# A selective scan on one core: order of the Softplus pair, place of the projections and of C

## The chip, the cores and the metric

The kernel runs on one core of a Trainium2 chip. A core has a TensorE for matrix products (PE in the profile; PEld is its weight load), a VectorE (DVE), a ScalarE (ACT), a GpSimd (POOL) and a SyncE (SP), which here only issues DMAs. Each engine works through its own list of instructions in order and waits at semaphores for the others. The metric is the time of the program on the device in microseconds (us).

## The reference

The input is `x` of shape (8, 384, 64, 64) in float32: 8 images of 384 channels. Two layers follow each other, both as `x = x + layer(group_norm(x))`.

- Layer 0 is a channel attention: three 1x1 convolutions and depthwise 3x3 convolutions for q, k and v, an attention between the channels of each of 8 heads, and an output projection.
- Layer 1 is a selective scan over the 4096 pixels in four directions (k = 0 to 3: by rows, by columns, and both reversed). The part that matters here, for each direction:

```python
x_dbl = jnp.einsum('bkdl,kcd->bkcl', xs, x_proj_weight)
dts, Bs, Cs = (x_dbl[:, :, :R], x_dbl[:, :, R:R + N], x_dbl[:, :, R + N:])   # R = 12, N = 16
dts = jnp.einsum('bkrl,kdr->bkdl', dts, dt_projs_weight)
dt = jax.nn.softplus(dts + dt_projs_bias[None, :, :, None])
# for each pixel, with 16 states for each of 384 channels:
dA = jnp.exp(dtt[..., None] * A)
h = h * dA + (dtt * ut)[..., None] * bt[:, :, None, :]
y = jnp.einsum('bkdn,bkn->bkd', h, ct)
```

The four directions are added, with a skip term `D * u`; a layer norm over the channels and a GELU end the layer.

## The kernel before

One image after the other, in three stages: `channel_attention`, `selective_scan`, `finish`. Only the scan is changed.

**Steps, pairs and periods.** A scan runs 32 steps for an image: 4 directions of 8 chunks of 512 pixels. In each step the 16 states are handled as 8 pairs (p = 0 to 7). The Python function `period(g)` writes the instructions of one pair; g counts pairs over all steps, so s = g // 8 is the step and p = g % 8 the pair. All instructions of the scan are pinned: on each engine they stand in the order in which the Python code writes them.

**What a period does.** Channels lie on the 128 partitions in three blocks (j = 0, 1, 2).

- ScalarE makes the decay `exp(dt * A)` for each of two states and three blocks: six `decay` instructions (line 449), each into one of two PSUM banks (`da`).
- GpSimd makes the input term `w * B`: two `drive` instructions (line 456), each for three blocks, one period ahead, from rows of B that `fetch` broadcast from DRAM three periods ahead.
- VectorE runs six `scan` instructions of 512 pixels (line 468). A decay bank comes free when the scan that read it has ended.
- TensorE turns the states of the pair before, so that pixels lie on partitions: eight `turn` groups of three 128x128 transposes (line 490), into the two banks of pool `ps_t`.
- Each turned block is multiplied by C and copied to SBUF by `apply_c` (lines 502 and 504). Most copies are on ScalarE; those in the set `on_dve` are on VectorE. A copy frees the bank that the transposes two further need.
- TensorE adds the copies up over pairs and states with `add_up`: three groups of four 384-column products (line 524), and a fourth group of twelve 128-column products (line 530), written one period later. In direction 0 the second pair adds the skip products as well (line 516).

**What a step needs besides.** `project(s, j)` makes dt, B and C for a chunk with three products of 512 columns into the one bank of pool `ps_m` (line 362); `lay_out` copies the result to SBUF (`xd`, line 370), writes B and C to DRAM and reads C back as rows (`cx`, eight DMAs on SP). `mingle_c` reorders `cx` on GpSimd, `turn_c` transposes it on TensorE into the bank of `ps_m` (`pct`, line 391), and `keep_c` copies it to SBUF on ScalarE (`ct`, line 399). The copies of the step's first pair read `ct`. In pair 1, called the burst, `step_matmuls` makes the inputs of Softplus for the next step: `pd` 0 into the bank of `ps_m`, `pd` 1 and 2 into the two banks of `ps_t` (line 416). `step_size` then runs three Softplus instructions on ScalarE (line 427), with a table load before and after them. `weigh` multiplies x by dt on GpSimd in pairs 2 to 4. In pair 1 VectorE also takes the finished sum of the step before (`take`), and SP stores it.

**Where these stand before.** The burst has copies 4, 5 and 6 on VectorE; pairs 4 and 7 have copy 3 there. Projections for step s + 2 stand in pairs 4, 5 and 6, between the second sum and transposes 6; `lay_out` of step s + 2 stands in pair 7. For step s + 1, `mingle_c` is in pair 2, `turn_c` in pair 3 and `keep_c` in pair 4.

[...]`ps_y` holds three (`py`), `ps_a` two (`da`), `ps_t` two, `ps_m` one.

Of the kernel before, what the change touches and what calls it, by code (L numbers as in the profile page):

```python
# [17 lines left out]
NJ = C // P  # L18
H = W = 64
L = H * W  # L20
CH = 512
# [8 lines left out]
XR = R + 2 * N  # L30
# [40 lines left out]
def tile_channel_attention_then_selective_scan(ctx: ExitStack, tc: tile.TileContext, a: dict):  # L71
# [224 lines left out]
    def selective_scan(b, x1, stats1):  # L296
# [10 lines left out]
        with ExitStack() as st:  # L307
# [8 lines left out]
            wx = wp.tile([P, NJ, K, XR], F32, name=f"wx{b}")  # L316
            nc.sync.dma_start(wx, a["x_proj"])

            with tc.tile_pool(name=f"sn{b}", bufs=1) as np_:
# [4 lines left out]
                for c in range(NCH):  # L324
                    for j in range(NJ):
                        s = x1[j][:, bass.ts(c, CH)]
# [11 lines left out]
            def view(t, k, c):  # L338

                if k % 2 == 0:  # L340
                    return t[:, bass.ts(c, CH)].rearrange("p (x y) -> p x y", y=W)
                return t.rearrange("p (h w) -> p w h", w=W)[:, bass.ts(c, CH // H), :]

            def split(t):
                return t.rearrange("p (x y) -> p x y", y=W)
# [5 lines left out]
            S = len(steps)  # L351
            wdts, pxs, xds, bc_ds, cts, dts, ws, bts = {}, {}, {}, {}, {}, {}, {}, {}

            def project(s, j):

                k, c = steps[s][:2]
                if j == 0:
                    if k not in wdts:
                        wdts[k] = work.tile([R, C], F32, tag="wdt", name=f"wdt{b}_{k}")
                        nc.sync.dma_start(wdts[k], a["dt_proj"][:, k, :])  # L360
                    pxs[s] = ps_m.tile([P, CH], F32, tag="m", name=f"px{b}_{s}")
                pin(nc.tensor.matmul(  # L362
                    split(pxs[s][:XR, :]), lhsT=wx[:, j, k, :], rhs=view(x1[j], k, c),
                    start=j == 0, stop=j == NJ - 1,
                ))

            def lay_out(s):

                xd = work.tile([XR, CH], F32, tag="xd", name=f"xd{b}_{s}")
                pin(nc.scalar.copy(xd, pxs.pop(s)[:XR, :]))  # L370
                bc_d = dram.tile([2 * N, CH], F32, tag="bcd", bufs=3, name=f"bcd{b}_{s}")
                nc.sync.dma_start(bc_d, xd[R:, :])

                cx = work.tile([NP * NQ, 2, HP], F32, tag="cx", name=f"cx{b}_{s}")
                for p in range(NP):
                    nc.sync.dma_start(
                        cx[p * NQ : (p + 1) * NQ],
                        bc_d[N + 2 * p : N + 2 * p + 2, :].rearrange("v (q l) -> q v l", l=HP),
                    )
                xds[s], bc_ds[s], cts[s] = xd, bc_d, cx  # L380
# [7 lines left out]
            def turn_c(s):  # L388

                pct = ps_m.tile([P, CH], F32, tag="m", name=f"pct{b}_{s}")  # L390
                pin(nc.tensor.transpose(
                    pct[:, : NP * NQ], cts[s].rearrange("r l v -> r (l v)"),
                    ident[: NP * NQ, : NP * NQ],
                ))
                cts[s] = pct

            def keep_c(s):
                ct = work.tile([P, NP * NQ], F32, tag="ct", name=f"ct{b}_{s}")
                pin(nc.scalar.copy(ct, cts[s][:, : NP * NQ]))
                cts[s] = ct  # L400
# [21 lines left out]
            def step_size(s, pds):  # L422
                k = steps[s][0]
                dts[s] = work.tile([P, NJ, CH], F32, tag="dt", name=f"dt{b}_{s}")
                ws[s] = work.tile([P, NJ, CH], F32, tag="w", name=f"w{b}_{s}")
                for j in range(NJ):
                    pin(nc.scalar.activation(  # L427
                        dts[s][:, j, :], pds[j], AF.Softplus, bias=small["dt_bias"][:, j, k : k + 1]
                    ))
# [147 lines left out]
                    move_y(s, t, True)  # L577

            for s in range(2):
                for j in range(NJ):  # L580
                    project(s, j)
                lay_out(s)
                if s == 0:
                    step_size(0, step_matmuls(0))
                    for j in range(NJ):
                        weigh(0, j)
                    for g in range(3):
                        fetch(g)
                    drive(0, 0)
                    drive(0, 1)  # L590
                    decay(0, 0, 0)
                    decay(0, 0, 1)
            mingle_c(0)
            turn_c(0)
            keep_c(0)

            def period(g):

                o, s, p = g - 1, g // NP, g % NP
                last = g == S * NP
                burst = p == 1 and s + 1 < S
                on_dve = {4, 5, 6} if burst else {3} if p in (4, 7) else set()
                taken = s - 1 if p == 1 and s > 0 else None

                def step(i):  # L610
                    if not last:
                        scan(g, *divmod(i, NJ))

                def next_decay(i):
                    if not last:
                        decay(g, *divmod(i + 2, NJ))

                def apply(q):
                    if o >= 0:
                        apply_c(o, q, nc.vector if q in on_dve else nc.scalar)  # L620

                def turned(q):
                    if o >= 0:
                        turn(o, q)

                def added(lb):
                    if o >= 0:
                        add_up(o, lb)

                def take_all():  # L630
                    if taken is not None:
                        for i in range(NJ):
                            take(taken, i)

                if not last:
                    h2s[g] = work.tile([P, NJ, CH, 2], F32, tag="h", bufs=3, name=f"h{b}_{g}")
                    if p == 2:
                        sum_of(s)
                if o >= 0:
                    keep_last(o)  # L640
                fetch(g + 3)
                drive(g + 1, 0)
                if p == 2 and s + 1 < S:
                    mingle_c(s + 1)
                if 2 <= p < 2 + NJ and s + 1 < S:
                    weigh(s + 1, p - 2)
                turned(0)
                turned(1)
                if o >= 1:
                    add_up(o - 1, NJ)  # L650
                apply(0)
                turned(2)
                step(0)
                next_decay(0)
                apply(1)
                turned(3)
                step(1)
                if not burst:
                    if p == 1:
                        take_all()  # L660
                    added(0)
                next_decay(1)
                apply(2)
                if burst:
                    pds = step_matmuls(s + 1)
                else:
                    turned(4)
                step(2)
                drive(g + 1, 1)
                next_decay(2)  # L670
                apply(3)
                if burst:
                    step_size(s + 1, pds)
                    step(3)
                    step(4)
                    take_all()
                    turned(4)
                    turned(5)
                    added(0)
                    apply(4)  # L680
                    turned(6)
                    apply(5)
                    turned(7)
                    added(1)
                    apply(6)
                    next_decay(3)
                    next_decay(4)
                    added(2)
                    step(5)
                    apply(7)  # L690
                    next_decay(5)
                    return
                turned(5)
                added(1)
                if 4 <= p < 4 + NJ and s + 2 < S:
                    project(s + 2, p - 4)
                if p == 7 and s + 2 < S:
                    lay_out(s + 2)
                if p == 3 and s + 1 < S:
                    turn_c(s + 1)  # L700
                if p == 4 and s + 1 < S:
                    keep_c(s + 1)
                apply(4)
                turned(6)
                step(3)
                next_decay(3)
                apply(5)
                turned(7)
                step(4)
                added(2)  # L710
                next_decay(4)
                apply(6)
                step(5)
                next_decay(5)
                apply(7)
# [51 lines left out]
    for b in range(B):  # L767
        x1, x1_d, stats1 = channel_attention(b)
# [51 lines left out]
```

## Time and profile before

| | before |
|---|---|
| time, median of 3 runs | 22354.12 us (22353.34 to 22354.86) |
| profiled execution, span | 22346.0 us |
| TensorE busy | 19355.1 us, 87% |
| VectorE busy | 19274.5 us, 86% |
| ScalarE busy | 17586.5 us, 79% |
| GpSimd busy | 15744.1 us, 70% |
| one scan instruction, VectorE (line 468, with a carry) | 1267 ns |
| one decay, ScalarE (line 449) | 700 ns |
| one copy, ScalarE (line 502) / VectorE (line 504) | 584 ns / 608 ns |
| one Softplus (line 427) / table load | 685 ns / 1283 ns |
| one projection product (line 362), two passes of 512 columns | 831 ns in the mean |

How to read it: the durations of following instructions on one engine overlap, so what an instruction costs its engine is the distance from start to start, which is shorter than its duration. Busy shares are over the whole span, which has three different stages for each image. In lists of groups and in the timeline, the bracket at the end is idle time of the engine just before the row, and what ended it. The stretch lists give, for each stretch, its length and the busy time (and count) of PE, PEld, DVE, ACT and POOL, then the granted TensorE clock, the DMA share and GB/s.

### The profile page before, as it was taken

To read this page: it belongs to the slowest core of one execution; us is meant where nothing else is said; L and a number is where in the kernel's file an instruction comes from. 1 tells how busy PE (TensorE), PEld (TensorE's weight loads), DVE (VectorE), ACT (ScalarE), POOL (GpSimd) and SP (SyncE) were. 2 spreads that over 40 slices of the span, in tenths; PEclk is the share of its full clock that TensorE was granted. 3 is DMA by queue.
4 is the path that set the end of the run, shared out by engine and by line. 5 is a ranking of instruction groups with operands and counts; after the bars stand their busy time and mean duration, and the time that the engine had idled before them with its cause. 6 is when DMAs were issued, how large, how long until landed. Compare 5 with 4: busy or idle time off the path is not lost.

```text
span 22346.0 us, 308970 instructions
## 1 busy us (share of the span) xinstructions
PE 19355.1 (87%) x113712; PEld 10323.1 (46%) x113712; DVE 19274.5 (86%) x16838; ACT 17586.5 (79%) x30794; POOL 15744.1 (70%) x7117
## 2 busy tenths in 40 slices
PE   7999879998799987999879998799987999879998
PEld 3544445444454444544445444454444544445444
DVE  7889878898789987889878998789987899878998
ACT  3999839998399983999839998399983999839998
POOL 0888718887188871888718887188871888718887
PEclk8999989999899998999989999899998999989999
DMA  1222312223122231222312223122231222312223
GB/s 51 77 86 86 109 46 77 86 87 109 46 78 85 87 113 43 77 86 86 113 43 77 86 87 113 42 78 85 87 114 42 77 85 87 114 41 77 86 86 103
DMA packets 872157, 1807.27 MB, mean 81 GB/s; under 512 B 123504, under 2 KB 513264, under 8 KB 861424
## 3 DMA queue, kind: packets, MB, share of 16 engines
q1 hardware_dynamic: 808464, 1658.85, 23.2%
q10 hardware_dynamic: 62176, 128.66, 1.7%
q8 instruction: 896, 14.68, 0.3%
q14 instruction: 621, 5.09, 0.1%
HBM read 1468.39 MB, written 318.77 MB: 80 GB/s over the span
## 4 chain that ended last, share of the span: by engine, by line
ACT 54%; PE 31%; DVE 10%; issue 3%; DMA 2%; POOL 1%; SPq 0%; ACTq 0%; POOLq 0%; DVEq 0%
ACT hc L502 27%; ACT da L449 23%; PE pt L490 10%; PE py L524 7%; PE px L362 4%; DVE v L196 4%; DVE ak L196 3%; PE pp L286 2%; ACT L427 1%; ACT dt L427 1%; DVE h L468 1%; PE py L530 1%; PE pa L245 1%; PE ptq L214 1%; PE py L516 1%
## 5 line engine op out<-in xcount | busy, mean ns | idle before, releaser
L456 POOL TENSOR_TENSOR db<-w,B 128x1536 f32<-128x1536 f32 x4096 | 14136.4, 3456 | 707.1 <-DVE h L468 476.4
L468 DVE TENSOR_TENSOR_SCAN h<-da,ca,db 128x512 f32<-128x512 f32 x10752 | 13047.4, 1267 | 870.5 <-ACT da L449 757.9
L502 ACT ACTIVATE hc<-pt,ct 128x384 f32<-128x384 f32 x15128 | 8531.9, 584 | 1179.8 <-PE pt L490 1147.9
L490 PE MATMUL pt<-ident,h 128*128 128x128 f32 x49152 | 8222.4, 293 | 1354.6 <-ACT hc L502 985.1
L449 ACT ACTIVATE da<-dt,neg_a 128x512 f32<-128x512 f32 x12288 | 8582.7, 700 | 211.7 <-DVE h L468 203.3
L490 PEld LDWEIGHTS pt<-ident,h 128*128 128x128 f32 x49152 | 5346.4, 144 | 6834.0 <-ACT hc L502 4194.0
L524 PE MATMUL py<-hc,pair 128*64 128x384 f32 x24576 | 5511.6, 532 | 10.2 <-DVE ys L575 10.2
L434 POOL TENSOR_TENSOR w<-x,dt 128x512 f32<-128x512 f32 x768 | 1074.8, 1400 | 3847.9 <-DMA cx<-bcd 3368.2
L468 DVE TENSOR_TENSOR_SCAN h<-da,db 128x512 f32<-128x512 f32 x1536 | 1786.8, 1212 | 298.3 <-ACT da L449 212.6
L524 PEld LDWEIGHTS py<-hc,pair 128*64 128x64 f32 x24576 | 1288.7, 140 | 1185.6 <-issue 1148.9
L530 PE MATMUL py<-hc,pair 128*64 128x128 f32 x24576 | 1796.1, 281 | 0.0
L530 PEld LDWEIGHTS py<-hc,pair 128*64 128x64 f32 x24576 | 1301.5, 136 | 343.4 <-issue 331.5
L482 POOL COPY ca<-h 128x6 f32<-128x6 f32 x1792 | 338.2, 189 | 1522.7 <-DVE h L468 1514.8
L504 DVE TENSOR_SCALAR hc<-pt,ct 128x384 f32<-128x384 f32 x1256 | 763.2, 608 | 623.8 <-PE pt L490 618.9
L362 PE MATMUL px<-x,wx 128*44 128x512 f32 x1536 | 1137.7, 831 | 28.9 <-ACT x L328 28.9
L416 PE MATMUL pd<-xd,wdt 12*128 12x512 f32 x1536 | 765.1, 632 | 5.8 <-ACT xd L370 5.8
L286 PE MATMUL pp<-v,mT 128*128 128x512 f32 x1152 | 527.2, 619 | 276.2 <-DVE v L196 276.2
L133 ACT ACT_TABLE_LOAD x16 | 20.5, 1283 | 892.4 <-DVE rstd L132 821.5
L764 POOL TENSOR_TENSOR o<-o,xr 128x512 f32<-128x512 f32 x192 | 310.3, 1645 | 504.8 <-DVE y L749 436.0
L757 PE MATMUL pz<-ident,y 128*128 128x128 f32 x768 | 160.8, 393 | 467.8 <-DVE y L749 291.6
L427 ACT ACTIVATE dt<-pd,dt_bias 128x512 f32<-128x512 f32 x768 | 475.4, 685 | 23.0 <-PE pd L416 19.5
L286 PEld LDWEIGHTS pp<-v,mT 128*128 128x128 f32 x1152 | 227.7, 199 | 574.4 <-issue 538.3
(234 smaller groups left out, 10873.2 us busy)
## 6 DMA issues: line engine op xcount, KB each, us to landing
B<-bcd SPq DMA_DIRECT2D x2048, 512.0 KB
yd<-ys SPq DMA_DIRECT2D x128, 576.0 KB
ys<-yd SPq DMA_DIRECT2D x256, 288.0 KB
yd<-ys SPq DMA_DIRECT2D x256, 288.0 KB
x<-in_x SPq DMA_DIRECT2D x24, 2048.0 KB
x1d<-x ACTq DMA_DIRECT2D x192, 256.0 KB
y<-yd SPq DMA_DIRECT2D x64, 768.0 KB
xr<-x1d ACTq DMA_DIRECT2D x64, 768.0 KB
```

The source lines that it names most:

```text
L196: nc.vector.scalar_tensor_tensor(o, pre3[:, y0 + dy : y1 + dy, x0 + dx : x1 + dx], dw[:, m, tap : tap + 1], o, ALU.mult, ALU.add,)
L286: nc.tensor.matmul(pc, lhsT=mT[:, j, bass.ts(m, P)], rhs=v[:, j, bass.ts(c, CH)], start=j == 0, stop=j == NJ - 1,)
L362: pin(nc.tensor.matmul(split(pxs[s][:XR, :]), lhsT=wx[:, j, k, :], rhs=view(x1[j], k, c), start=j == 0, stop=j == NJ - 1,))
L427: pin(nc.scalar.activation(dts[s][:, j, :], pds[j], AF.Softplus, bias=small["dt_bias"][:, j, k : k + 1]))
L434: pin(nc.gpsimd.tensor_mul(split(ws[s][:, j, :]), view(x1[j], k, c), split(dts[s][:, j, :])))
L449: pin(nc.scalar.activation(t, dts[s][:, j, :], AF.Exp, scale=neg_a[:, j, k, n : n + 1]))
L456: pin(nc.gpsimd.tensor_mul(t, ws[g // NP], bts[g][:, v : v + 1, :].broadcast_to([P, NJ, CH])))
L468: pin(nc.vector.tensor_tensor_scan(h, da, db, 0.0 if start else carries[s - 1][:, j, n : n + 1], ALU.mult, ALU.add,))
L490: pin(nc.tensor.transpose(t[:, bass.ts(j, P)], h2s[g][:, j, bass.ts(q, HP), :].rearrange("p l v -> p (l v)"), ident))
L502: pin(eng.activation(out, src, AF.Copy, scale=scale))
L524: pin(nc.tensor.matmul(py[f * HP : (f + 1) * HP, lb, :C], lhsT=pair, rhs=hc[:, f, :], **flags))
L530: pin(nc.tensor.matmul(py[f * HP : (f + 1) * HP, j, C:], lhsT=pair, rhs=hc[:, f, bass.ts(j, P)], **flags,))
```

## The change

Softplus runs in the order 1, 2, 0. The burst has four copies on VectorE (4 to 7), which stand one after the other with the last three transpose groups, and all three sums follow the last transposes. Each projection is cut into two products of 256 columns; the six pieces stand in pairs 2 to 7, behind the third sum. `lay_out` moves from pair 7 to pair 0 of the next step, `mingle_c` from pair 2 to pair 3, and `turn_c` and `keep_c` to pair 0 of the step that reads them. Copy 3 goes to VectorE in pair 0, and no longer in pairs 4 and 7. In each step VectorE has five copies, as before.

```diff
-            def project(s, j):
+            def project(s, i):
+                j, f = divmod(i, 2)
                 k, c = steps[s][:2]
-                if j == 0:
+                if i == 0:
...
+                part = slice(f * CH // W // 2, (f + 1) * CH // W // 2)
                 pin(nc.tensor.matmul(
-                    split(pxs[s][:XR, :]), lhsT=wx[:, j, k, :], rhs=view(x1[j], k, c),
-                    start=j == 0, stop=j == NJ - 1,
+                    split(pxs[s][:XR, :])[:, part, :], lhsT=wx[:, j, k, :],
+                    rhs=view(x1[j], k, c)[:, part, :], start=i == 0, stop=i == 2 * NJ - 1,
                 ))
...
-                for j in range(NJ):
+                for j in (1, 2, 0):
                     pin(nc.scalar.activation(
                         dts[s][:, j, :], pds[j], AF.Softplus, bias=small["dt_bias"][:, j, k : k + 1]
                     ))
...
             mingle_c(0)
-            turn_c(0)
-            keep_c(0)
...
-                on_dve = {4, 5, 6} if burst else {3} if p in (4, 7) else set()
+                on_dve = {4, 5, 6, 7} if burst else {3} if p == 0 else set()
...
-                if p == 2 and s + 1 < S:
+                if p == 3 and s + 1 < S:
                     mingle_c(s + 1)
...
                     take_all()
                     turned(4)
                     turned(5)
-                    added(0)
                     apply(4)
                     turned(6)
                     apply(5)
                     turned(7)
-                    added(1)
                     apply(6)
+                    apply(7)
+                    for lb in range(NJ):
+                        added(lb)
                     next_decay(3)
                     next_decay(4)
-                    added(2)
                     step(5)
-                    apply(7)
                     next_decay(5)
                     return
                 turned(5)
                 added(1)
-                if 4 <= p < 4 + NJ and s + 2 < S:
-                    project(s + 2, p - 4)
-                if p == 7 and s + 2 < S:
-                    lay_out(s + 2)
-                if p == 3 and s + 1 < S:
-                    turn_c(s + 1)
-                if p == 4 and s + 1 < S:
-                    keep_c(s + 1)
+                if p == 0 and 0 < s < S - 1:
+                    lay_out(s + 1)
                 apply(4)
                 turned(6)
                 step(3)
...
                 turned(7)
                 step(4)
                 added(2)
+                if p >= 2 and s + 2 < S:
+                    project(s + 2, p - 2)
+                if p == 0 and s < S:
+                    turn_c(s)
                 next_decay(4)
                 apply(6)
+                if p == 0 and s < S:
+                    keep_c(s)
                 step(5)
                 next_decay(5)
                 apply(7)
```

More of the change, by code (lines that the diff above doesn't have):

```diff
@@ L579, in selective_scan @@
             for s in range(2):
-                for j in range(NJ):
-                    project(s, j)
+                for i in range(2 * NJ):
+                    project(s, i)
                 lay_out(s)
```

## The prediction, made before the changed kernel had run

> **What bounds the kernel now.** I read the page's busy shares first, then the chain, then one scan step cut into its eight pairs, then the order of work inside two of those pairs. TensorE, VectorE and ScalarE all look full, and the chain alternates between ScalarE and TensorE:
>
> ```profile
> PE 19355.1 (87%) x113712; PEld 10323.1 (46%) x113712; DVE 19274.5 (86%) x16838; ACT 17586.5 (79%) x30794; POOL 15744.1 (70%) x7117
> ...
> ACT 54%; PE 31%; DVE 10%; issue 3%; DMA 2%; POOL 1%; SPq 0%; ACTq 0%; POOLq 0%; DVEq 0%
> ```
>
> So no engine's sum decides; the hand-over does. The scan takes about 2204 us of each image's 2793 (first scan to last); the change touches nothing else. A stretch list of one step of image 3 (direction 2), cut where VectorE starts pairs 0 to 7 (length first, TensorE's granted clock third from the end):
>
> ```profile
> 10262.72:10270.03 7.31, 6.50 (x50) 3.70 (x48) 7.23 (x8) 7.31 (x15) 7.07 (x3) 1.00 0.26 87
> 10270.03:10283.11 13.08, 11.42 (x59) 5.55 (x58) 10.80 (x14) 11.43 (x18) 7.04 (x3) 0.87 0.41 139
> 10283.11:10290.22 7.11, 6.14 (x47) 3.62 (x48) 7.11 (x7) 7.00 (x13) 6.97 (x5) 1.00 0.39 115
> 10290.22:10297.65 7.43, 6.86 (x49) 3.72 (x47) 7.27 (x8) 7.43 (x15) 7.43 (x5) 1.00 0.22 72
> 10297.65:10305.52 7.87, 7.72 (x54) 4.18 (x54) 7.68 (x9) 7.70 (x15) 7.87 (x5) 1.00 0.21 67
> 10305.52:10312.83 7.31, 6.82 (x45) 3.27 (x44) 7.23 (x8) 7.15 (x14) 7.31 (x4) 1.00 0.22 74
> 10312.83:10321.01 8.18, 7.70 (x51) 3.97 (x52) 7.37 (x7) 7.55 (x14) 8.18 (x4) 1.00 0.20 64
> 10321.01:10329.53 8.52, 8.05 (x58) 4.46 (x58) 7.79 (x8) 8.04 (x15) 8.07 (x4) 1.00 0.16 63
> ```
>
> The floor is about 7.3. Pair 1 loses 6 us (Softplus); pairs 6 and 7 about 1 us each (projections).
>
> I name the work of a period: copies c0 to c7 (`hc`), exponentials e0 to e5 (`da`), transposes T0 to T7 (`pt`), sums Y0 to Y2 and Y3 (`py`). ScalarE issues c0 e0 c1 e1 c2 e2 c3 c4 e3 c5 e4 c6 e5 c7: an exponential holds it 0.61 us and a copy 0.47 (start to start in the trace), so 6 x 0.61 + 8 x 0.47 = 7.4. I measure periods from c0 to c0. TensorE in pair 5:
>
> ```profile
> 10310.59 0.55 PE L490 MATMUL pt<-ident,h 128*128 128x128 f32 x3 [0.28 <-ACT hc L502]
> 10311.07 0.87 PE L524 MATMUL py<-hc,pair 128*64 128x384 f32 x4
> 10311.77 1.02 PE L362 MATMUL px<-x,wx 128*44 128x512 f32 x2
> 10312.72 0.87 PE L490 MATMUL pt<-ident,h 128*128 128x128 f32 x6
> 10313.52 0.87 PE L524 MATMUL py<-hc,pair 128*64 128x384 f32 x4
> 10314.32 0.55 PE L490 MATMUL pt<-ident,h 128*128 128x128 f32 x3
> ```
>
> These are T5, Y1, a projection, T6 and T7, Y2, the next T0. T5 waits for c3's bank, and the next c0 starts 0.58 after T0. The loop is c0 to c3 3.23, to T5 0.63, to Y1 0.48, to px 0.70, to T6 0.95, to Y2 0.80, to T0 0.80, to c0 0.58: 8.17, as measured (8.18). Without px, Y1 to T6 is 0.80, and the loop is 7.32, just under ScalarE's 7.38.
>
> Pair 1, TensorE, then the ScalarE lines around Softplus:
>
> ```profile
> 10273.60 2.84 PE L416 MATMUL pd<-xd,wdt 12*128 12x512 f32 x6
> 10277.80 1.54 PE L490 MATMUL pt<-ident,h 128*128 128x128 f32 x6 [1.36 <-ACT dt L427]
> 10279.27 1.55 PE L524 MATMUL py<-hc,pair 128*64 128x384 f32 x4
> 10280.75 0.92 PE L490 MATMUL pt<-ident,h 128*128 128x128 f32 x6
> ```
>
> ```profile
> 10275.19 1.28 ACT L427 ACT_TABLE_LOAD   x1
> 10276.48 1.84 ACT L427 ACTIVATE dt<-pd,dt_bias 128x512 f32<-128x512 f32 x3
> ```
>
> T4 waits 1.36 us for the second Softplus, since pd1 and pd2 sit in the transposes' two banks; and six transposes then take 1.54 instead of 0.87: half clock.
>
> [...]mean clock 0.87 in pair 1 alone, which is half clock for 3.4 us of 13.08 (6.8 in other steps). [...]The trace shows the 1283, and Softplus 1.29 after it[...].[...]
>
> **The change, part by part** (per step, c0 to c0).
>
> *Half pieces, p = 2 to 7.* Three projections of 0.95 (px to T6; 1.81 in directions 1 and 3, whose reads are strided) become six, and stand between Y2 and the next T0. [...]a half piece streams 0.43, so with 0.10 of switching T0 follows it by 0.53. Y2 to T0 grows from 0.80 to 0.70 + 0.53 = 1.23, and the loop from 7.32 to 7.75. Strided: (1.81 - 0.10)/2 + 0.10 = 0.96, loop 8.18. No trace shows a half piece: at least 0.33 (stream alone, its switch hidden), at most 0.60; I take 0.43. All six pay, because ScalarE has only 0.06 of slack. Also gone from here: the VectorE copy of pairs 4 and 7, the transposed C row (0.21) and its copy (0.34), and `xd` (0.47). Before, pairs 2 to 7 took 7.5, 7.6, 7.7, 8.2, 8.2, 7.7 = 46.8 (direction 2), or 49.3 where the next projection is strided; after, 6 x 7.75 = 46.5, or 6 x 8.18 = 49.1. With direction 0, where the skip products add about 1.3 to pair 2, the mean is -0.2 us.
>
> *Pair 0.* It gets the VectorE copy (c3), `xd`, and C's transpose and copy. ScalarE: e2 ends its slot at 3.23, xd to 3.70, c4, e3 at 4.20 (held by scan 3, which the VectorE copy pushes 0.51), c5 at 4.83. T7 at 5.45, Y2 at 5.87, C's transpose 0.79 later at 6.66, lasting 0.27: the copy `ct` can't start before 6.97. c6 was issued at 6.02, so ScalarE stands 0.5 us. Then e5 at 7.17, c7 7.78, next c0 8.25. Before: 7.38. +0.87 (bounds: 0.4 if C's transpose slips ahead of Y2's end, 1.0 if the copy also holds ScalarE its shown 0.34).
>
> *Pair 1.* The order (1, 2, 0) should free the first bank one Softplus (0.58) sooner. But the table load carries the wait for the first input, now pd1, the second of three products: it ends at 10274.99 + 0.59 = 10275.58, so the load moves from 10275.19 by 0.42. T4 gains only 0.15, and e3 and e4 start 0.42 later (hidden: scan 5 waits longer for VectorE's copies). From c0: T4 6.34, T5 6.98, VectorE's c4 7.28, c5 7.92; T6 no longer follows Y0, so T6 7.95, c6 8.89, T7 8.59, c7 9.53, scan 5 at 10.05 instead of 10.6. But Y0, Y1 and Y2 now all follow T7: 9.36 onward, 4.3 us at half clock (1.55 for four products less overlap), 2.1 at full. Before, Y0 lay beside the wait. The clock returns one or two windows after it fell[...]. In the early case T0 starts near 11.8, in the late one near 12.8; c0 0.6 later; both about equally often: 12.9 against a mean of 13.1 before. -0.2. Bounds: 12.0 (full clock from T7: Y0 to Y2 done at 11.3) and 13.8 (half clock to the end).
>
> *At nothing.* `mingle_c` and `weigh` on GpSimd: same work, mingle one period later; it has at least 1.4 us in hand at every `db`. SP: the write of B and C and eight `cx` loads move one period later, behind the same fetches; pair 1's fetch queues behind them, but its B is first used two periods on; next step's B rows are first fetched in pair 5. No load is on the path, at a DMA share of 0.2 to 0.4.
>
> Sum: +0.87 - 0.2 - 0.2 = +0.47 for 30 steps; step 30 (no projection, so -1.0) -0.35, step 31 +0.5. An image: 14.1 + 0.15 = 14.3; eight: +114. Against the profiled span 22346: 22460; the three timed runs have a median 8 us higher: **22468 us**, +0.5%. Two runs of this kernel differ by far less than 0.2% (45 us), which is about what a measurement can tell.
>
> **Rivals.**
>
> A, faster: the clock comes back by T7 (or never falls), so Y0 to Y2 take 2.1. Then pair 1 takes about 12.0 instead of 13.1: -1.1 + 0.87 - 0.2 = -0.43 a step, 22354 - 0.43 x 240 = 22250. For: half the steps have the early clock, and T6 and T7 are 1.3 us earlier. Against: the transposes are spread out with waits on VectorE[...]. It decides once pair 1 falls below about 12.4.
>
> B, no change: pair 1 gains 0.5 to 0.8, as much as pair 0 loses; 22354 within 45.
>
> C, much slower: half pieces pay full switching at both ends, 0.60 instead of 0.43: six times 0.17 is 1.0 a step, 22710.
>
> D, the copy `ct` finds its transpose early, so pair 0 costs only 0.4: 22350, in B's range. Against: C's transpose stands behind Y2, which needs c5.
>
> **Chances.** Forecast 0.60 (own range 22400 to 22570), A 0.22, B with D 0.13, C 0.05. Slower by over 0.2%: forecast and C, less a little of the forecast's low edge, 0.63; within 0.2%: 0.14; faster: 0.23. The range must reach into A and may leave out C: 22220 to 22640.
>
> **What would show it.** c0-to-c0 periods of 7.75 and 8.18 in pairs 3 to 7; a ScalarE wait of about 0.5 us before `ct`, named for the C transpose, and 8.25 in pair 0; the Softplus table load about 0.4 later after pair 1's c3; Y0 to Y2 in one row of 12 after T7, and a wait of ScalarE on `pt` at the next c0. The prediction fails if pair 1 is under 12.4, or if half pieces fit in slack and pairs 3 to 7 stay at 7.4.

## The result: slower by 0.67%

| | before | changed |
|---|---|---|
| median of 4 runs | 22353.73 us | 22505.42 us |
| range | 22353.3 to 22354.86 | 22497.53 to 22508.54 |
| ratio of the runs, 95% interval | 1 | 1.0067 [1.005, 1.0085] |
| profiled span | 22346.0 us | 22502.7 us |

The forecast was 22468 us. The profile after, by the views shown before. The chain has turned from ScalarE first to TensorE first:

```profile
PE 50%; ACT 35%; DVE 9%; issue 3%; DMA 1%; POOL 1%; SPq 0%; ACTq 0%; POOLq 0%; DVEq 0%
```

The stretch list of the same step of image 3, cut where VectorE starts each pair; shown are pairs 0, 1, 2, 5, 6 and 7:

```profile
10336.77:10344.87 8.10, 7.72 (x54) 4.01 (x52) 7.68 (x9) 7.88 (x15) 7.07 (x3) 1.00 0.20 67
10344.87:10357.92 13.05, 10.80 (x53) 5.88 (x51) 11.52 (x15) 10.87 (x18) 7.04 (x3) 0.77 0.45 142
10357.92:10366.20 8.28, 7.80 (x54) 4.15 (x52) 7.27 (x8) 6.81 (x13) 8.13 (x4) 0.95 0.37 109
...
10381.73:10389.49 7.76, 7.37 (x52) 3.96 (x52) 7.26 (x7) 7.54 (x15) 7.76 (x4) 1.00 0.23 71
10389.49:10397.26 7.77, 7.37 (x52) 3.98 (x52) 7.27 (x8) 7.54 (x15) 7.54 (x4) 1.00 0.21 67
10397.26:10405.02 7.76, 7.36 (x52) 3.96 (x52) 7.26 (x7) 7.54 (x15) 7.07 (x3) 1.00 0.20 68
```

Pair 0 went from 7.31 to 8.10 and pair 2 from 7.11 to 8.28; pairs 6 and 7 went from 8.18 and 8.52 to 7.8; pair 1 stayed. The same from c0 to c0, as the prediction counts, mean of steps 1 to 30 of image 0:

| pair | 0 | 1 | 2 | 3 | 4 | 5 | 6 | 7 | step |
|---|---|---|---|---|---|---|---|---|---|
| before | 7.39 | 13.11 | 7.83 | 7.62 | 8.12 | 8.65 | 8.65 | 7.63 | 69.01 |
| changed | 8.24 | 12.94 | 8.34 | 8.05 | 8.01 | 8.01 | 8.02 | 8.01 | 69.61 |

Over all images pair 1 is 13.08 before and 12.99 after, and the step is 0.68 longer: 0.68 x 30 x 8 = 163 us, against 152 in the times.

Pair 0, the ScalarE timeline around the copy `ct`:

```profile
10344.44 0.56 ACT L504 ACTIVATE hc<-pt,ct 128x384 f32<-128x384 f32 x1
10345.46 0.21 ACT L401 COPY ct<-pct 128x64 f32<-128x64 f32 x1 [0.46 <-PE pct L393]
```

ScalarE stands idle for 0.46 us until TensorE has transposed C, as forecast. A half piece in pair 3, TensorE's timeline (Y2, px, then the next T0 and T1):

```profile
10373.81 0.87 PE L526 MATMUL py<-hc,pair 128*64 128x384 f32 x4
10374.50 0.59 PE L364 MATMUL px<-x,wx 128*44 128x256 f32 x2
10375.03 0.96 PE L492 MATMUL pt<-ident,h 128*128 128x128 f32 x6
```

Y2 to T0 is 1.22, forecast 1.23. Pair 1, TensorE, then ScalarE's next c0:

```profile
10353.00 3.15 PE L492 MATMUL pt<-ident,h 128*128 128x128 f32 x12 [1.26 <-ACT dt L429]
10356.08 3.49 PE L526 MATMUL py<-hc,pair 128*64 128x384 f32 x12
10359.50 0.87 PE L492 MATMUL pt<-ident,h 128*128 128x128 f32 x6
```

```profile
10360.09 0.58 ACT L504 ACTIVATE hc<-pt,ct 128x384 f32<-128x384 f32 x1 [1.36 <-PE pt L492]
```

The four transpose groups T4 to T7 wait 1.26 us (1.36 before), then run together. The three sums are one row of 12 and take 3.42 us to the next transposes, mostly at half clock (0.60 in the mean of these 3.42 us). ScalarE waits 1.36 us for those.

### The profile page after: what moved, and what is told of

Same layout as the page of the kernel before. It is cut to its first block, busy times and chain, and to the rows that moved or that the text cites. A ratio compares the mean times of both kernels' runs of the same rounds, so it can differ in the third digit from the quotient of the medians.

```text
span 22502.7 us, 312049 instructions
## 1 busy us (share of the span) xinstructions
PE 19484.5 (87%) x115248; PEld 10552.0 (47%) x115248; DVE 19306.1 (86%) x16830; ACT 17528.0 (78%) x30802; POOL 15775.8 (70%) x7117
## 4 chain that ended last, share of the span: by engine, by line
PE 50%; ACT 35%; DVE 9%; issue 3%; DMA 1%; POOL 1%; SPq 0%; ACTq 0%; POOLq 0%; DVEq 0%
PE pt L492 18%; ACT hc L504 18%; PE py L526 15%; ACT da L451 14%; PE px L364 4%; DVE v L196 4%; DVE ak L196 3%; PE pd L418 2%; PE pp L286 2%; ACT L429 1%; PE py L532 1%; PE pa L245 1%; ACT dt L429 1%; PE py L518 1%; PE ptq L214 1%
## 5 line engine op out<-in xcount | busy, mean ns | idle before, releaser
L492 PE MATMUL pt<-ident,h 128*128 128x128 f32 x49152 | 8387.6, 296 | 1376.8 <-ACT hc L504 903.9
L504 ACT ACTIVATE hc<-pt,ct 128x384 f32<-128x384 f32 x15136 | 8666.3, 587 | 1032.3 <-PE pt L492 1024.0
L526 PE MATMUL py<-hc,pair 128*64 128x384 f32 x24576 | 5441.6, 530 | 10.2 <-DVE ys L577 10.2
L364 PE MATMUL px<-x,wx 128*44 128x256 f32 x3072 | 1262.2, 502 | 39.8 <-ACT x L328 28.9
L364 PEld LDWEIGHTS px<-x,wx 128*44 128x44 f32 x3072 | 378.8, 124 | 632.8 <-issue 579.6
```

The lines of the kernel that those rows point to most:

```text
L364: pin(nc.tensor.matmul(split(pxs[s][:XR, :])[:, part, :], lhsT=wx[:, j, k, :], rhs=view(x1[j], k, c)[:, part, :], start=i == 0, stop=i == ...
L492: pin(nc.tensor.transpose(t[:, bass.ts(j, P)], h2s[g][:, j, bass.ts(q, HP), :].rearrange("p l v -> p (l v)"), ident))
L504: pin(eng.activation(out, src, AF.Copy, scale=scale))
L526: pin(nc.tensor.matmul(py[f * HP : (f + 1) * HP, lb, :C], lhsT=pair, rhs=hc[:, f, :], **flags))
```

## The experiments

The theory has three parts. Pair 0 loses because C's transpose stands behind Y2. A piece of a projection costs its stream on a loop through c3, whether it is cut in halves or not. Pair 1 profits little, since its table load waits and TensorE's half clock stretches the sums. The rivals: the moved instructions cost their own time; half pieces are a loss or a gain in themselves; the order of pair 1 is a loss or a gain in itself. In the pieces of code, `...` marks lines left out, and most notes behind `#` are added for the reader.

### C's transpose ahead of the third sum

```diff
+                if p == 0 and s < S:
+                    turn_c(s)
                 added(2)
                 if p >= 2 and s + 2 < S:
                     project(s + 2, p - 2)
-                if p == 0 and s < S:
-                    turn_c(s)
```

> The changed kernel, with C's transpose in pair 0 ahead of the third sum instead of behind it. If pair 0 is long because the copy ct waits for that transpose behind Y2 (a ScalarE stall of about 0.5 us), pair 0 falls from 8.24 to about 7.8 us and the time to 22505 - 0.45 x 248 = 22395 us. If instead the instructions moved into pair 0 (xd, ct, the VectorE copy) set its length by their own time, pair 0 stays at 8.2 and the time at 22505.

Measured: 22298.92 us, ratio to before 0.9977 [0.9968, 0.9986]. ScalarE at the same place:

```profile
10251.38 0.56 ACT L504 ACTIVATE hc<-pt,ct 128x384 f32<-128x384 f32 x1
10251.85 0.20 ACT L401 COPY ct<-pct 128x64 f32<-128x64 f32 x1
```

The wait is gone and pair 0 is 7.66 instead of 8.24. So 0.58 of its loss of 0.85 was the wait. The other 0.27 stays, and there the rival is likely right: 7.66 is about what every pair with c3 on VectorE takes (7.64 in the runs further down). This one line's place decides whether the change loses or gains.

The time is 96 us under the forecast. Pair 0 gave 0.13 us a step more than I had said, and pair 1 fell from 12.99 to 12.79 (all images), though nothing in it changed. TensorE's clock records say why: in these three kernels pair 1 falls to half clock in all 240 steps counted, for 3.41 us or for 6.83 (one or two windows in the words of the prediction and the expectations). In steps 1 to 30 of all images (number of steps, and the mean length of pair 1 in us):

| | 3.41 us at half clock | pair 1 then | 6.83 us at half clock | pair 1 then |
|---|---|---|---|---|
| before | 127 | 12.70 | 113 | 13.51 |
| changed | 93 | 12.32 | 147 | 13.41 |
| C's transpose ahead | 144 | 12.34 | 96 | 13.45 |

The changed pair 1 is shorter than before in each case, by 0.37 and 0.11; but 6.83 us at half clock came in 61% of its steps, not in 47%. With the shares of before it would be 12.83. What sets these shares was not tried. They move a run's time by up to some tens of us, so I compare like steps below.

### The order of Softplus, and that of its products

```diff
-                for j in (1, 2, 0):      # Softplus
+                for j in range(NJ):
```

> The changed kernel with Softplus back in the order 0, 1, 2. If the table load waits for the first Softplus input, and so gives back with 1, 2, 0 most of what the order frees, going back makes T4 only 0.15 us later: 22505 + 0.15 x 248 = 22540 us, and the table load starts at once behind c3. If the order alone is worth a whole Softplus (0.57 us), it costs 0.57 x 248 = 140: 22645.

```diff
-                pds = []
-                for j in range(NJ):      # products, in step_matmuls
+                pds = {}
+                for j in (1, 0, 2):
...
-                    pds.append(pd)
+                    pds[j] = pd
```

> The changed kernel with the products for Softplus made in the order 1, 0, 2, so that the first Softplus input is also the first made. If the table load waits for product 1, it starts 0.42 us sooner after c3 (0.65 instead of 1.07), T4 to T7 with it, and pair 1 falls by about 0.4 us: 22505 - 0.4 x 248 = 22405 us. If the wait at the load is harmless, or pair 1 is set by the three sums at half clock and by the window alone, the time stays within 30 us of 22505.

Measured: 22536.2 us (1.0084 [1.0068, 1.0101]) with Softplus 0, 1, 2, and 22434.8 us (1.0039 [1.0024, 1.0054]) with products 1, 0, 2. The group of Softplus' table loads, first of the changed kernel, then with products 1, 0, 2 (busy, mean ns of one, then idle before them):

```profile
L429 ACT ACT_TABLE_LOAD x256 | 328.4, 1283 | 117.2 <-PE pd L418 116.9
```

```profile
L429 ACT ACT_TABLE_LOAD x256 | 328.4, 1283 | 42.6 <-PE pd L418 42.3
```

The load waited 117.2 / 256 = 0.46 us for product 1. In the kernel before, and with Softplus 0, 1, 2, ScalarE stands idle there for 4.5 and 4.6 us in all. So the new order gave with one hand and took with the other: going back costs 31 us, where a whole Softplus would have cost 140. Making product 1 first gains 71 us (100 forecast); the load still waits 0.17, because product 1 now needs the bank of T2 and waits for c2 (0.47 us of TensorE in step 20 of image 3).

In steps with 3.41 and with 6.83 us at half clock, pair 1 is 12.45 and 13.50 with Softplus 0, 1, 2, and 12.03 and 13.28 with products 1, 0, 2, against 12.32 and 13.41 in the changed kernel. So both differences hold in like steps.

### Whole projections in their old place

```diff
+                if 4 <= p < 4 + NJ and s + 2 < S:
+                    project(s + 2, p - 4)        # whole, behind added(1)
                 if p == 0 and 0 < s < S - 1:
                     lay_out(s + 1)
...
-                if p >= 2 and s + 2 < S:
-                    project(s + 2, p - 2)        # halves, behind added(2)
```

> The changed kernel with whole projections (512 columns) back between Y1 and T6 of pairs 4, 5 and 6; all else as changed. If every piece, half or whole, lengthens the loop c3, T5, Y1, T6, T7, Y2, T0, c0 by its own stream, pairs 4 to 6 take 8.17 (9.03 where the projection is strided), pairs 2, 3 and 7 take 7.4, and the sum is that of six half pieces within 0.2 us a step: 22505 within 40. If half pieces pay more at their ends, the whole ones gain about 1 us a step: 22260; if half pieces were hidden, whole ones lose 1.5 us or more a step: 22860.

Measured: 22554.56 us, 1.0092 [1.0077, 1.0107]; pairs 2 to 7 of image 0 are 7.74, 7.45, 8.69, 8.64, 8.66, 7.40, together 48.58, against 48.44 with halves. 49 us more is a little outside the 40 that I gave, and far from both rivals. Six halves and three wholes cost the same within 0.15 us a step. Pairs 3 and 7, without a piece, take 7.4.

### Copy 3 on VectorE, and where a piece then stands

If c3 is on VectorE, T5 need not wait for a copy on ScalarE. Three kernels use that:

```diff
-                on_dve = {4, 5, 6, 7} if burst else {3} if p == 0 else set()
+                on_dve = {4, 5, 6, 7} if burst else {3} if p != 1 else set()
```

> The changed kernel with copy 3 on VectorE in every pair but pair 1, the half pieces left behind Y2. ScalarE then has 0.47 us of slack in pairs 2 to 7. If the loop were ScalarE's work plus a piece, these pairs would fall to 7.66 (VectorE's bound: six scans and a copy) or 7.8: 22505 - 1.5 x 240 = 22150 us. If a piece behind Y2 sits on a second loop, through c5 (scan 3, pushed by VectorE's copy, holds e3, then c5 4.83, T7 5.45, Y2 5.93, px, T0 7.16, c0 7.74; 8.17 strided), nothing is gained: 22505 - 10, within 40.

```diff
# the same, C's transpose ahead, products 1, 0, 2, and:
+                if p >= 2 and s + 2 < S:
+                    project(s + 2, p - 2)        # halves, behind added(1)
                 if p == 0 and 0 < s < S - 1:
                     lay_out(s + 1)
```

> The changed kernel with copy 3 on VectorE in every pair but pair 1, the half pieces between Y1 and T6, C's transpose ahead of Y2, and the products for Softplus in the order 1, 0, 2. With copy 3 on VectorE, T5 comes at 3.30 instead of 3.86, so a strided half piece (0.96 to T6) still leaves T6 at 5.4 and c6 at 6.0, where ScalarE would be anyway: pairs 2 to 7 all at 7.66, strided or not. Against the run with C's transpose ahead: -0.1 to -0.6 a pair, on average 1.8 us a step, and 0.25 from the products: 22299 - 2.05 x 240 = 21810 us. If the pieces cost their stream wherever they stand, it stays at 22240.

```diff
# the kernel before, and:
-                on_dve = {4, 5, 6} if burst else {3} if p in (4, 7) else set()
+                on_dve = {4, 5, 6} if burst else {3} if p in (4, 5, 6, 7) else set()
```

> The kernel before, with copy 3 on VectorE in pairs 5 and 6 too (whole projections in pairs 4 to 6 as before). Pair 4 of before has both and takes 7.65 (8.49 strided); if the VectorE copy is the reason, pairs 5 and 6 fall from 8.18 to 7.65 and from 9.04 to 8.49, 1.1 us a step: 22350 - 1.1 x 240 = 22090 us. If pair 4 is short because it is the first of the three and the delay only arrives later, pairs 5 and 6 stay and VectorE's copies add to them: 22350 to 22450.

| | time | ratio to before | pair 5, strided projection |
|---|---|---|---|
| c3 on VectorE, halves behind Y2 | 22459.5 | 1.0049 [1.0034, 1.0064] | 8.17 |
| c3 on VectorE, halves before T6, with the two moves above | 21782.3 | 0.9745 [0.973, 0.9759] | 7.7 |
| before, c3 on VectorE in pairs 4 to 7 | 22065.08 | 0.9873 [0.9858, 0.9887] | 8.49 |

All three came out within 36 us of the forecast. A strided pair, first with the halves behind Y2, then before T6:

```profile
10771.32:10779.49 8.17, 7.71 (x54) 3.98 (x50) 7.69 (x9) 7.45 (x14) 8.02 (x4) 1.00 0.22 67
```

```profile
10444.11:10451.75 7.64, 7.44 (x52) 3.96 (x52) 7.64 (x8) 7.33 (x14) 7.64 (x4) 1.00 0.23 72
```

VectorE (the third busy time) has the same work in both. In the second it is busy from end to end, so the piece no longer adds to the pair. The copy itself has a price: in step 30, which has no pieces, pairs 3 to 7 take 7.64 with c3 on VectorE and 7.4 without.

### The Softplus pair alone, and the first sum back

```diff
# the kernel before, and:
-                for j in range(NJ):                                  # Softplus
+                for j in (1, 2, 0):
-                on_dve = {4, 5, 6} if burst else {3} if p in (4, 7) else set()
+                on_dve = {4, 5, 6, 7} if burst else {3} if p in (4, 7) else set()
...                 # and all three sums behind turned(7), as in the change
```

> The kernel before with only the Softplus pair changed: Softplus 1, 2, 0, four copies on VectorE, the three sums behind T7. Projections, C and pairs 0 and 2 to 7 as before. If pair 1 in the changed kernel is 13.0 against 13.1 by its own doing, it is 13.0 here too: 22351 - 0.1 x 248 = 22330 us, within 40. If pair 0 of the changed kernel, which ends later, had eaten a gain of pair 1, it falls to 12.4 here: 22180. If the pair is a loss by itself, it is over 22390.

```diff
# the changed kernel, and in the burst:
                     turned(5)
+                    added(0)
                     apply(4)
...
-                    for lb in range(NJ):
+                    for lb in range(1, NJ):
                         added(lb)
```

> The changed kernel with the first sum of pair 1 back between T5 and T6. If moving all three sums behind T7 gained scan time but no TensorE time (the slow clock is paid on the sums in either place), pair 1 stays at 13.0 within 0.2 and the time within 50 us of 22505. If the three sums behind T7 are the loss, it gets 0.5 us a step faster (22385); if getting T6 and T7 out earlier is a gain, 0.5 slower (22625).

Both missed. The pair alone: 22257.4 us, 0.996 [0.9945, 0.9975], a gain of 90 us where 20 were forecast. Pair 1 is 12.85 and pair 2 is 7.74 instead of 7.83. In steps with 3.41 us at half clock pair 1 is 12.47 (12.70 before), with 6.83 it is 13.52 (13.51), and the 3.41 came in 152 of 240 steps instead of 127. So about half of the gain in pair 1 is the shares, and which of the three moves in this run makes the rest is open.

The first sum back: 22583.4 us, 78 slower than the changed kernel where 50 was the limit, although 3.41 us at half clock came in 141 steps. In those pair 1 grew to 13.00 (12.32 changed); with 6.83 it is 13.43 (13.41). So getting T6 and T7 out ahead of the first sum is a gain, 78 us or 0.33 a step, and it lies in the steps with 3.41 us at half clock.

### TensorE's clock

If the half clock is the price of pair 1, it should be possible to take it away. The products for Softplus read 12 rows (`12*128 12x512` in the profile before), the transposes 128 (`128*128`). That the rows matter to the clock was a guess. Here both operands are read over 128: the weights are zeros beyond row 12; the input has B and C in rows 13 to 44, which meet zero weights, and zeros beyond. The result and the columns streamed are the same:

```diff
-                        wdts[k] = work.tile([R, C], F32, tag="wdt", name=f"wdt{b}_{k}")
+                        wdts[k] = wdp[k % 2]      # [P, C], zeros beyond row R
...
-                xd = work.tile([XR, CH], F32, tag="xd", name=f"xd{b}_{s}")
+                xd = xdp[s % 2]                   # [P, CH], zeros beyond row XR
...
-                        pd, lhsT=wdts[k][:, bass.ts(j, P)], rhs=xds[s][:R, :], start=True, stop=True
+                        pd, lhsT=wdts[k][:, bass.ts(j, P)], rhs=xds[s], start=True, stop=True
```

On the best version so far, on the kernel before, and on the changed kernel:

> The best version so far (copy 3 on VectorE outside pair 1, pieces between Y1 and T6, C's transpose ahead of Y2, products 1, 0, 2), with the Softplus products over all 128 rows of the array: weights and inputs are padded with zeros, their time is the same. [...]TensorE stays at full clock in more than half of the pairs 1, which then take 11.6 instead of 12.6 in the mean of these: 21782 - 0.6 x 240 = 21640 us, and fewer half-clock windows of two in a row. If rows don't count, 21782 within 30.

> The kernel before with the Softplus products over all 128 rows (zeros beside the 12), nothing else. If the half clock is the price of pair 1 before the change too, pair 1 falls from 13.1 to about 11.2 (T4 6.5 after c0, T7 8.5, scan 5 at 9.3, e5 10.5, c0 11.2 at full clock): 22351 - 1.9 x 248 = 21880 us, and no half-clock window is left in pair 1. If the full-row products only help where T6 and T7 stand directly behind T5, it stays over 22100.

> The changed kernel with the Softplus products over all 128 rows, nothing else. With the clock out of the way pair 1 is set by T4 6.34, T7 8.2, scan 5 at 9.5, e5 10.8, c0 11.4: 22505 - 1.6 x 248 = 22110 us, so 230 slower than the kernel before with the same products. If the changed order of pair 1 gains by itself and only the clock's windows ate it, pair 1 is 11.0 or less, and the distance falls to 130 or less.

| full rows on | time | ratio to before | the same kernel without full rows |
|---|---|---|---|
| best version | 21454.26 | 0.9601 [0.9585, 0.9617] | 21782.3 |
| before | 21936.95 | 0.9815 [0.9799, 0.9831] | 22351.82 |
| changed | 22141.35 | 0.9906 [0.9892, 0.9921] | 22505.42 |

Pair 1 of the best version, TensorE, then the whole stretch:

```profile
9867.15 2.84 PE L423 MATMUL pd<-xdp,wdp 128*128 128x512 f32 x6 [0.47 <-ACT hc L509]
9870.39 2.39 PE L497 MATMUL pt<-ident,h 128*128 128x128 f32 x12 [0.40 <-ACT dt L434]
9872.71 2.16 PE L531 MATMUL py<-hc,pair 128*64 128x384 f32 x12
```

```profile
9863.23:9874.74 11.51, 10.10 (x58) 4.97 (x54) 11.35 (x14) 10.66 (x18) 7.06 (x3) 1.00 0.45 145
```

The products take the same 2.84 us, but the clock is 1.00 over the stretch (0.77 over pair 1 of the changed kernel), and the twelve products of the sums take 2.16 us instead of the 3.49 shown for the changed kernel. In steps 1 to 30 no pair 1 of this run or of the kernel before with full rows is at half clock at any time. The best version gained more than forecast (21640), the other two a little less (21880 and 22110).

With full rows the changed kernel loses 204 us to the kernel before (230 forecast). Pair 0 (8.23 against 7.39) is the loss; pair 1 is equal in the mean of all images (11.43 against 11.39). But full rows did not hold the clock everywhere: in the changed kernel pair 1 still fell to half clock in 29 of 240 steps and took 12.78 there. In the other 211 it takes 11.24, so at full clock the changed order gains 0.15 us, and the 29 steps eat it.

## Why the prediction was right

The waits and loops forecast are the ones seen. The middle of the forecast was 37 us low, and two terms of the sum were mis-sized: pairs 2 to 7 and pair 1, by about 0.1 us a step each.

- **Pair 0, +0.87.** Measured +0.85, and the wait at `ct` 0.46 for 0.5. Moving the transpose alone took 0.58 of it away.
- **Half pieces, 7.75 and 8.18.** Measured 7.76 and 8.19 in directions 2 and 3, 7.82 and 8.25 in 0 and 1. The two passes of a half piece start 0.22 us apart in the trace (0.41 strided), those of a whole projection before 0.43 (0.84). The price of 0.43, taken between 0.33 and 0.60, was right.
- **Pairs 2 to 7, -0.2.** Measured -0.08. The term is a small difference of two sums. In direction 2 the sum before is 46.68 where 46.8 was read (the six lengths listed there add up to 46.9), and the sum after is 46.59 where 46.5 was forecast: -0.09 instead of -0.3. In direction 0 nothing is gained at all (+0.03). The skip products stand on the loop in pair 2 just before Y1 and Y2, and the piece comes on top: 9.22 (9.64 with a strided piece), where before it was 8.87 (8.82). TensorE there:

```profile
9247.16 0.83 PE L518 MATMUL py<-skip,x 128*128 128x128 f32 x6
9247.92 0.87 PE L526 MATMUL py<-hc,pair 128*64 128x384 f32 x4
9248.62 0.59 PE L364 MATMUL px<-x,wx 128*44 128x256 f32 x2
```

- **Pair 1, -0.2.** Measured -0.09. The late table load (0.42 forecast, 0.46 measured) and the wait of c0 on the transposes are there. The early and late cases (3.41 and 6.83 us at half clock), c0 at 12.4 and 13.4, measured 12.32 and 13.41. What failed is "both about equally often": the late one came in 61% of the steps, which is worth 0.12 us.
- **Rival A** needed pair 1 under about 12.4 with the clock back by T7. The mean is 12.99; only the 93 steps with 3.41 us at half clock, at 12.32, lie just under that. **Rival B** needed a gain of 0.5 to 0.8 in pair 1. **Rival C** (0.60 for a half piece) is excluded by the 1.22 measured from Y2 to T0, since it needs 1.40. **Rival D** is what happens when the transpose is moved ahead of Y2 (22298.92, pair 0 +0.27), and not in the change as it stands.

## What to carry to other kernels

When three engines hand work around a loop, price a move by the loop that it lengthens. Behind the third sum a half piece made a pair 0.36 us longer, or 0.79 strided (7.76 and 8.19, against 7.4 without). Before T6, once one copy was on another engine, it added nothing to speak of in pairs 4 to 7 (7.61 to 7.70, against 7.64 without). Before a consumer is moved to the head of its queue, look at the order in which its inputs are made, and at what waits in its name (here a table load). And a small instruction, such as a 64-column transpose, can hold a full engine for half a microsecond (0.46 us at `ct`) if it stands behind long work that it doesn't need.

## What the runs showed of the hardware

In all 240 steps counted of the kernel before, and in all 240 of the changed one, TensorE's clock fell to half in pair 1, for 3.41 or 6.83 us; the mean clock of the profiled runs is 0.928 and 0.927. In 82 steps of the changed kernel the 3.41 us before the fall hold the products for Softplus whole (at least 2.8 of their 2.84 us), and the clock fell all the same.

With these products read over 128 rows, zeros included, pair 1 was at half clock in none of the 240 steps of the best version and of the kernel before, and in 29 of 240 of the changed kernel; the mean clock of the three profiled runs is 0.958, 0.957 and 0.956. In the best version the products took the same 2.84 us. What makes the clock fall or come back was not shown.

Full rows gave 364 and 415 us on the changed kernel and the one before, and 328 on the best version. Other paddings were not tried.
